# Layer 3 of a four-layer graph network: the projection by seven half-width products for each pair of graphs, and attention scores masked in place

## The chip, the core and the metric

The kernel runs on one core of one Trainium2 chip, in one launch, with no arithmetic on the host. The metric is the device time of that core in microseconds (us), taken as the median of several runs. Engines are named as the profile names them: PE is the matrix engine (TensorE) and PEld its weight loads, DVE is VectorE, ACT is ScalarE, POOL is GpSimd, SP is the engine that issues most of the DMAs.

## The reference

`x` holds 128 graphs of 128 nodes with 256 features (f32), `adj` their 128x128 adjacency (here only 0 and 1). Four layers follow one another, and each ends in `x = layernorm(x + layer(x, adj))`:

```
layer 0: four scores  (x * a_k) @ x.T  chosen by adj == 1..4, leaky relu, softmax, @ x
layer 1: relu(x @ W_upd + mean over incoming edges of (x @ W_msg) + bias)
layer 2: three GRU steps; each: m = h @ weight[i]; aggr = A.T @ m; h = gru_cell(aggr, h)
layer 3: Wh = h @ W                                  # W is 256x256
         e  = leaky_relu(Wh @ a1 [:, None] + Wh @ a2 [None, :])
         alpha = softmax(where(adj > 0, e, -1e9)); out = elu(alpha @ Wh)
```

The change lies in layer 3.

## The kernel before

**Tiling.** The 128 graphs go through in 32 groups of `G = 4`. A tile holds the four graphs of a group; features come in `KC = 2` chunks of 128. For each group the Python code records all operations of `loading`, `layer0`, `layer1`, `gru` (three steps) and `layer3`. It issues none of them at once: each record is an `Op` with its engine, its buffers and what it must follow. Every instruction is therefore issued from one line (L232 in the profile), and groups in the profile are told apart by the names of their tiles.

**The planner.** After recording, a list scheduler (lines 1064 to 1163) simulates the five engines with fixed costs (`pe_cost`, `dve_cost` and so on) and at each moment picks, among the operations that can start, the one with the earliest due time. Due times come from `paced`: the group's number times `PERIOD`, plus the stage's entry in `TIMES`, plus corrections for the first six groups (`HEAD`) and the last six (`TAIL`). `EAGER` and `RUSH` move single operations forward, `HOP`, `PE_HOP`, `SLACK` and `DMA_SLACK` are the delays that it assumes between an operation and its consumer. What comes out is only an order for each engine's queue. On the chip each engine follows its queue strictly, so an operation that isn't ready holds up all that stands behind it on its engine. Several groups are under way at once: while one is in layer 3, later ones are in layer 0, in layer 1 and in the GRU.

**Buffers.** Tiles with the same tag share memory (`tile_of(tag, ..., bufs)`). Eight PSUM banks exist: four under `ps`, four under `gate`. `LENT` and `LAST` let the first and the last groups use tags that stand idle then.

**Products of f32 data** are two passes on PE, each with its own weight load, so the profile counts two matmuls where the code has one. Two parts of the kernel already replace eight block products by seven: the GRU's gates (`gate`, with sums made by `sums`) and layer 1 (lines 701 to 736). There one PSUM region `sums` is built up by successive products, and between two of them an ACT or DVE instruction copies the state so far (`snapshot`). The next product onto `sums` has to wait for that copy.

**Layer 3 before.** `w3x` is 128 x 2 x 258: for each chunk the two columns W@a1 and W@a2 and the 256 columns of W, all with their mean over the features taken off, so that only the scale of the preceding layer norm is left to apply. For each graph two matmuls of 258 columns add up in one bank (line 964), and one ACT instruction multiplies by `rstd` and writes `wh` (line 968). `rstd` comes from `statistics(x3)`: `bn_stats` and `bn_aggr` on DVE, then POOL's power -0.5 (tile `norm`); `x3` is the same data in the other orientation, brought through DRAM, so PE can make the products before `rstd` is there. Column 1 of `wh` is turned into rows through DRAM (tile `e`); ACT's leaky relu adds column 0; POOL fills a second tile `alpha3` with -1e9, and DVE copies `e` into it where `m_gt` (adj > 0) is set. Softmax, the product with `wh`, elu, residual and the final layer norm follow.

The last group (`end`) is taken in two halves and gets its rows by a PE transpose instead of DRAM.

Of the kernel before, what the change touches and what calls it, by code (L numbers as in the profile page):

```python
# [9 lines left out]
U8 = mybir.dt.uint8  # L10
# [8 lines left out]
def kernel(  # L19
# [266 lines left out]
    def sp_cost(op, n, out, ins, pointers, sums):  # L286
# [7 lines left out]
    engines = (PE, DVE, ACT, POOL, SP)  # L294


    PERIOD = 80.86253
    EAGER, RUSH = 5.0884, 1.2432
    HOP, PE_HOP, SLACK, DMA_SLACK = 0.1014, 0.0400, 0.1471, 0.9854
    STAGES = ("loading", "layer0", "layer1", "step0", "step1", "step2", "layer3")  # L300
    TIMES = {
        "loading": ((-258.6487, -221.2981), (-177.7494, -380.8362),),
        "layer0": ((-168.3552, -133.3064), (-133.3096, -106.9608),),
        "layer1": ((-54.7884, -31.0927), (-31.3632, 1.9381),),
        "step0": ((1.0169, 6.5128), (2.0472, 18.0997), (16.3112, 40.9206),),
        "step1": ((47.0157, 58.4871), (54.6617, 81.1755), (64.0140, 96.5891),),
        "step2": ((103.0883, 125.4009), (124.8396, 134.0628), (117.2682, 150.2660),),
        "layer3": ((180.1358, 214.4429), (215.7571, 242.5671),),
        "weights": ((-169.3721, -63.5307), (-339.2026, -166.3094), (66.3971, -238.7909), (-41.6293, -259.0106), (11.0405, -48.3179), (-169.5807, -0.3718), (-340.4637, 8.4156),),
    }  # L310
    HEAD = (
        (-117.215, -459.664, -34.333, -29.161, 1.563, 32.989, 16.116),
        (1.845, -18.257, -21.556, 24.853, 21.190, -0.454, 36.615),
        (-212.928, -33.522, 22.746, 10.256, 10.342, 13.022, 18.440),
        (-257.587, 42.115, 8.229, 7.910, 18.207, 9.248, -2.588),
        (-39.284, 3.397, 16.065, 1.469, 3.447, 5.718, 2.966),
        (-103.261, -31.186, -1.392, -17.316, -0.422, 9.872, 6.232),
    )
    TAIL = (
        (218.880, -30.061, -19.516, -24.870, -14.301, 14.485, 9.628),  # L320
        (355.667, -8.045, -0.184, 12.567, 6.874, -3.896, -23.536),
        (108.002, 3.414, -6.453, -11.126, -2.010, -5.080, -2.710),
        (401.812, -59.141, -23.770, -14.732, -25.938, -6.000, 51.631),
        (550.661, -48.436, -51.059, -2.941, 57.600, 48.509, 200.181),
        (353.049, 27.888, 2.032, 49.745, 45.095, 76.448, 165.620),
    )

    def spread(start, end, pe_only=False):
# [31 lines left out]
    ident = tile_of("ident", [P, P])  # L360
    ident.buf.tile = ident_tile
    neg_half = tile_of("neg_half", [P, G])

    hu_tiles = [work.tile([P, 2 * D + 1], F32, tag=f"hu{k}", name=f"hu{k}") for k in range(2)]
    for hu_tile in hu_tiles:
# [9 lines left out]
    c_gi = tile_of("c_gi", [P, NL, KC, 3 * D])  # L375

    w3x = tile_of("w3x", [P, KC, 2 + D])

    w_ul = tile_of("w_ul", [P, 3, D])
    w_sh = tile_of("w_sh", [P, 3, 3, P])  # L380
# [2 lines left out]
    def weights():  # L383

        POOL.memset(neg_half, -0.5)
        nats, wnat = [], []
        for src, tag, bufs in ((w_ih, "hT", 6), (w_hh, "rest", 4)):
            for g in range(0, NGC, 2):
# [110 lines left out]
                PE.matmul(ps[:, : 2 + D], mean, w3x[:, c, :], start=(c == 0), stop=(c == KC - 1))  # L499
        for c in range(KC):  # L500
            DVE.tensor_sub(w3x[:, c, :], w3x[:, c, :], ps[:, : 2 + D])
        early(6)


# [67 lines left out]
    def softmax(alpha, tag, quick, tile=tile_of):  # L572

        n = alpha.shape[1]
        nmax = tile_of(f"nmax_{tag}", [P, n], 2)
        DVE.tensor_reduce(nmax, alpha, AX.X, OP.max, negate=True)
        rs = tile_of(f"rsum_{tag}", [P, n], 2)
        for b in range(n):
            ACT.activation(
                alpha[:, b, :], alpha[:, b, :], AF.Exp, bias=nmax[:, b : b + 1], scale=1.0,  # L580
                accum_out=rs[:, b : b + 1],
            )
        rinv = tile_of(f"rinv_{tag}", [P, n], 2)
# [110 lines left out]
    def layer1(g, s):  # L694
        x1, a_f, xT = s.x1, s.a_f, s.x1T

        s.m_gt = tile_of("m_gt", [P, G, N], 3, U8)
        POOL.tensor_scalar(s.m_gt, a_f, 0.0, None, op0=OP.is_gt)
        s.a_ne = tile_of("a_ne", [P, G, N], 3, BF16)
        DVE.tensor_scalar(s.a_ne, a_f, 0.0, None, op0=OP.not_equal)  # L700
        t = tile_of("xd", [P, 2, 3, N])
# [69 lines left out]
    def gru(g, s):  # L771
# [166 lines left out]


    LAST = {  # L940
        "wh": ("x_in", 1), "e": ("alpha0", 1), "alpha3": ("x_blocks", 1),
        "probT_3": ("probT_0", 1), "xd": ("x1T", 1),
    }

    def layer3(g, s, first, last):


        n = last - first
        end = g == NG - 1
        names = LAST if first else {}  # L950
        two, three = ("2b", "3b") if first else ("2", "3")

        def tile(tag, shape, bufs=1):
            tag, bufs = names.get(tag, (tag, bufs))
            return tile_of(tag, shape, bufs)

        x3 = s.x3 if n == G else s.x3[:, first:last]
        shift, rstd = statistics(x3, two)
        wh = tile("wh", [P, n, 2 + D])
        for b in range(n):  # L960
            ps = bank()
            with PE:
                for c in range(KC):
                    PE.matmul(
                        ps[:, : 2 + D], s.rT[c][:, (first + b) * N : (first + b + 1) * N], w3x[:, c, :],
                        start=(c == 0), stop=(c == KC - 1),
                    )
            ACT.mul(wh[:, b, :], ps[:, : 2 + D], rstd[:, b : b + 1])


        f = tile("e", [P, 4 * n, 32])
        e = f.rearrange("p (k b) c -> p b k c", [P, n, 4, 32], b=n)
        if end:
            ps = bank()
# [3 lines left out]
            rows = [ps[:, b * N : (b + 1) * N].rearrange("p (k c) -> p k c", c=32) for b in range(n)]  # L978
        else:
            z = tile_of("z_f", [P, 32])  # L980
            DVE.transpose(z, wh[:, :, 1:9])
            way = tile_of("way_f", [16, 32], 4, F32, dram)
            SP.dma_start(out=way, in_=z.rearrange("(m r) c -> r m c", [8, 16, 32], r=8)[0])
            SP.dma_start(out=f, in_=way.partition_broadcast(P))
            rows = [e[:, b] for b in range(n)]
        alpha = tile("alpha3", [P, n, N])
        POOL.memset(alpha, NEG3)
        for b in range(n):
            leaky(e[:, b], rows[b], wh[:, b, 0:1])
        BLOCKS = "p b (k c) -> p b k c"  # L990
# [201 lines left out]
```

## Time and profile before

| | |
|---|---|
| median of 3 runs | 2675.43 us (2675.09 to 2675.49) |
| the profiled execution | 2673.91 us |
| its span, first to last instruction | 2672.1 us |
| mean granted TensorE clock | 0.997 of full |
| PE / PEld busy | 2626.9 us (98%) / 2265.7 us (85%) |
| DVE / ACT / POOL busy | 2216.7 (83%) / 1790.2 (67%) / 1659.3 us (62%) |
| layer-3 projection, 480 of its f32 passes | 124.3 us busy as a group |
| mean DMA rate | 107 GB/s |

Durations below come from the profiled execution. The profile's *busy* of PE counts from a matmul's start to its modelled end, and matmuls overlap in the array, so a row's mean (381 ns for a pass of 256 columns) is longer than the distance at which such passes follow each other. That distance has to be read from start times in the timeline. "Idle before" is the time that an engine stood still before a group's instructions, with what ended it.

### The profile page before, as it was taken

Reading aid. Unit: us, or ns where it says so; the run is one execution under the profiler, and the core shown is the slowest. Engines: PE = TensorE matmul, PEld = TensorE weight load, DVE = VectorE, ACT = ScalarE, POOL = GpSimd, SP = SyncE. Lnnn points to the kernel's source line nnn. Section 1 sums busy time; section 2 is a strip of 40 time slices with the busy share of each in tenths; the row PEclk is TensorE's granted clock in tenths of the full one; section 3 lists DMA queues with packets and bytes.
Section 4 is the critical chain, followed back from the end, with each engine's and each line's share of the span. In section 5 each row is a group of like instructions: output and inputs, shape, how many; then the busy total and the mean of one; then the engine's idle time right before and its main releaser. Section 6 shows DMA issues by size and latency. Waiting matters only on the chain.

```text
span 2672.1 us, 44288 instructions
## 1 busy us (share of the span) xinstructions
PE 2626.9 (98%) x13700; PEld 2265.7 (85%) x13700; DVE 2216.7 (83%) x5386; ACT 1790.2 (67%) x4330; POOL 1659.3 (62%) x1536
## 2 busy tenths in 40 slices
PE   8999999999999999999999999999999999999996
PEld 6788888888888888888888888888888888888885
DVE  6887888888888888888888898888898888888877
ACT  4555766666776676776676766666776677657666
POOL 6456666655676655676665676656666656666452
PEclk9999999999999999999999999999999999999999
DMA  6545544555555555555555555555554545435431
GB/s 138 106 86 103 123 96 106 120 102 111 117 117 111 113 106 115 108 116 112 112 110 114 107 115 113 110 112 115 107 123 103 111 103 120 108 75 109 92 82 45
DMA packets 1317389, 286.83 MB, mean 107 GB/s; under 512 B 1068193, under 2 KB 1313057, under 8 KB 1317153
## 3 DMA queue, kind: packets, MB, share of 16 engines
q1 hardware_dynamic: 1314704, 281.63, 51.0%
q10 hardware_dynamic: 2448, 2.36, 0.4%
q8 instruction: 110, 1.80, 0.3%
q14 instruction: 127, 1.03, 0.1%
HBM read 168.44 MB, written 115.41 MB: 106 GB/s over the span
## 4 chain that ended last, share of the span: by engine, by line
PE 90%; DVE 5%; ACT 2%; DMA 1%; issue 1%; SPq 1%; POOL 0%; POOLq 0%; ACTq 0%; DVEq 0%
PE gate L232 62%; PE ps L232 28%; SPq L232 1%; DVE z L232 0%; DVE st L232 0%; DVE t_m L232 0%; DVE t_d L232 0%; ACT xs L232 0%; ACT xb L232 0%; DVE rest L232 0%; DVE xb L232 0%; DVE hu L232 0%; DVE alpha L232 0%; DVE t_z L232 0%; DVE xd L232 0%
## 5 line engine op out<-in xcount | busy, mean ns | idle before, releaser
L232 POOL TENSOR_TENSOR t_r<-t_r,t_i 128x512 f32<-128x512 f32 x186 | 244.4, 1326 | 204.5 <-ACT t_i L232 167.2
L232 PE MATMUL gate<-t_h,w_hhT 128*128 128x256 f32 x1152 | 343.8, 381 | 3.1 <-ACT t_z L232 2.3
L232 PE MATMUL gate<-t_h,w_sh 128*128 128x256 f32 x1152 | 338.8, 382 | 1.8 <-ACT q L232 0.5
L232 PE MATMUL gate<-hT,w_hhT 128*128 128x256 f32 x1152 | 336.6, 383 | 1.1 <-ACT x_in L232 0.6
L232 POOL TENSOR_TENSOR t_h<-hT 128x256 f32<-128x256 f32 x188 | 145.4, 791 | 308.4 <-DVE hT L232 241.0
L232 PE MATMUL gate<-t_m,c_gi 128*128 128x256 f32 x1116 | 331.6, 379 | 0.0
L232 PE MATMUL gate<-t_m,w_sm 128*128 128x256 f32 x1116 | 328.2, 379 | 0.1
L232 PE MATMUL gate<-agT,c_gi 128*128 128x256 f32 x1116 | 326.3, 380 | 0.5 <-ACT t_r L232 0.2
L232 POOL TENSOR_TENSOR t_d<-hT,t_n 128x512 f32<-128x512 f32 x192 | 260.2, 1366 | 40.1 <-ACT t_n L232 38.4
L232 ACT ACTIVATE q<-gate,bhn 128x256 f32<-128x256 f32 x372 | 176.7, 475 | 126.8 <-PE gate L232 120.8
L232 PE MATMUL ps<-xs,xT 128*128 128x256 f32 x1024 | 242.9, 381 | 5.4 <-ACT xs L232 5.4
L232 PEld LDWEIGHTS gate<-t_h,w_sh 128*128 128x128 f32 x1152 | 213.2, 190 | 40.9 <-ACT t_r L232 5.5
L232 PEld LDWEIGHTS gate<-t_h,w_hhT 128*128 128x128 f32 x1152 | 215.6, 190 | 37.3 <-ACT t_z L232 4.5
L232 PEld LDWEIGHTS gate<-hT,w_hhT 128*128 128x128 f32 x1152 | 213.7, 190 | 36.4 <-DVE t_i L232 4.8
L232 PEld LDWEIGHTS gate<-t_m,w_sm 128*128 128x128 f32 x1116 | 211.6, 190 | 29.9 <-ACT t_i L232 0.8
L232 PEld LDWEIGHTS gate<-t_m,c_gi 128*128 128x128 f32 x1116 | 211.3, 190 | 30.2 <-ACT t_i L232 1.2
L232 PEld LDWEIGHTS gate<-agT,c_gi 128*128 128x128 f32 x1116 | 210.6, 190 | 30.7 <-ACT agT L232 1.4
L232 POOL TENSOR_TENSOR norm<-norm,neg_half 128x4 f32<-128x4 f32 x128 | 157.2, 1228 | 111.1 <-DVE norm L232 76.6
L232 PEld LDWEIGHTS ps<-xs,xT 128*128 128x128 f32 x1024 | 194.2, 191 | 34.6 <-ACT xs L232 7.7
L232 ACT COPY t_r<-gate 128x256 f32<-128x256 f32 x279 | 103.1, 369 | 177.8 <-PE gate L232 177.5
L232 POOL TENSOR_SCALAR mk<-a_f 128x512 uint8<-128x512 f32 x120 | 186.6, 1564 | 7.0 <-DVE alpha L232 3.3
L232 ACT COPY t_z<-gate 128x256 f32<-128x256 f32 x288 | 105.8, 367 | 126.1 <-PE gate L232 124.4
(265 smaller groups left out, 7035.0 us busy)
## 6 DMA issues: line engine op xcount, KB each, us to landing
way<-z SPq DMA_DIRECT2D x188, 256.0 KB, 2.5
way_h<-z SPq DMA_DIRECT2D x126, 256.0 KB, 2.4
hn<-way_h SPq DMA_DIRECT2D x504, 64.0 KB, 2.5
x_blocks<-in_x_dram SPq DMA_DIRECT2D x248, 64.0 KB, 2.4
x_in<-in_x_dram SPq DMA_DIRECT2D x31, 512.0 KB, 4.2
way_p<-z SPq DMA_DIRECT2D x62, 256.0 KB, 2.4
probT<-way_p SPq DMA_DIRECT2D x248, 64.0 KB, 2.4
xc<-way SPq DMA_DIRECT2D x124, 128.0 KB, 3.0
```

The lines of the kernel that those rows point to most:

```text
L232: getattr(self.engine, name)(*[a.real() if isinstance(a, View) else a for a in args], **{k: a.real() if isinstance(a, View) else a for k, ...
```

## The change

For all groups but the last, the eight products of 258 columns in a group become fourteen of 129 (`M3 = 1 + D // 2`). For two graphs and two chunks, the activations form a 2x2 block matrix `a11, a12, a21, a22` (graph, chunk), and the two halves of `w3x` another. Four POOL instructions for each group form sums of activations in a tile under the tag `xd` (the fourth overwrites `a21` in `rT`); four DVE instructions in `weights` form sums of weights once, in `w3s`. For each pair of graphs, seven matmuls write two banks. Four ACT instructions take `sums` out at four states, each scaled by `rstd`, straight into `wh`; three DVE instructions add the other products, scaled too. Three of the four ACT instructions stand between two matmuls onto `sums`.

The scores lose their second tile: `alpha3` and POOL's filling of it go; the mask is turned round (`m_no`, adj <= 0), and DVE writes -1e9, broadcast from a small tile `neg3`, into `e` itself. Softmax then works on `e`, whose rows lie in blocks of 32 (except in the last group). The tables and constants of the planner have other values. With them the order of all queues can change.

```diff
-    PERIOD = 80.86253
-    EAGER, RUSH = 5.0884, 1.2432
-    HOP, PE_HOP, SLACK, DMA_SLACK = 0.1014, 0.0400, 0.1471, 0.9854
+    PERIOD = 80.11372
+    EAGER, RUSH = 2.6344, 0.7143
+    HOP, PE_HOP, SLACK, DMA_SLACK = 0.0400, 0.1378, 0.0735, 0.0000
...
@@ weights
+        DVE.memset(neg3[0], NEG3)
...
+        b11, b12, b21, b22 = [w3x[:, c, e : e + M3] for c in range(KC) for e in (0, M3)]
+        DVE.tensor_sub(w3s[:, 0], b12, b11)
+        DVE.tensor_sub(w3s[:, 1], b22, w3s[:, 0])
+        DVE.tensor_sub(w3s[:, 2], b22, b12)
+        DVE.tensor_sub(w3s[:, 3], b21, w3s[:, 1])
@@ softmax
-        DVE.tensor_reduce(nmax, alpha, AX.X, OP.max, negate=True)
+        DVE.tensor_reduce(nmax, alpha, AX.X if len(alpha.shape) == 3 else AX.XY, OP.max, negate=True)
@@ layer1
-        s.m_gt = tile_of("m_gt", [P, G, N], 3, U8)
-        POOL.tensor_scalar(s.m_gt, a_f, 0.0, None, op0=OP.is_gt)
+        s.m_no = tile_of("m_no", [P, G, N], 3, U8)
+        POOL.tensor_scalar(s.m_no, a_f, 0.0, None, op0=OP.is_le)
@@ layer3
-        for b in range(n):
-            ps = bank()
...
-            ACT.mul(wh[:, b, :], ps[:, : 2 + D], rstd[:, b : b + 1])
+        if end:
+            for b in range(n):
+                ps = bank()
...
+                ACT.mul(wh[:, b, :], ps[:, : 2 + D], rstd[:, b : b + 1])
+        else:
+            pairs = [r.rearrange("p (h j n) -> p h j n", [P, 2, 2, N], h=2, j=2) for r in s.rT]
+            a11, a12, a21, a22 = [pairs[c][:, :, j] for j in range(2) for c in range(KC)]
+            t = tile_of("xd", [P, 3, 2, N])
+            POOL.tensor_add(t[:, 0], a21, a22)
+            POOL.tensor_sub(t[:, 1], t[:, 0], a11)
+            POOL.tensor_sub(t[:, 2], a12, t[:, 1])
+            POOL.tensor_sub(a21, a11, a21)
+            for h in range(2):
+                shared, other = bank(), bank()
+                sums, second, third = shared[:, :M3], shared[:, M3 : 2 * M3], other[:, :M3]
+                data = [[pairs[c][:, h, j] for c in range(KC)] for j in range(2)]
...
+                def scaled(cols, j, half, rush=0.0):
+                    b = 2 * h + j
+                    ACT.mul(wh[:, b, half * M3 : (half + 1) * M3], cols, rstd[:, b : b + 1])
+                    ops[-1].rush = rush
+
+                def more(cols, j, half):
+                    b = 2 * h + j
+                    part = wh[:, b, half * M3 : (half + 1) * M3]
+                    DVE.scalar_tensor_tensor(part, cols, rstd[:, b : b + 1], part, op0=OP.mult, op1=OP.add)
+
+                product(sums, data[0][0], w3x[:, 0, :M3], first=True)
+                scaled(sums, 0, 0, 1.0)
+                product(second, data[0][1], w3x[:, 1, :M3], last=True)
+                product(sums, t[:, 1, h], w3s[:, 1])
+                scaled(sums, 0, 1, 1.0)
+                more(second, 0, 0)
+                product(third, t[:, 0, h], w3s[:, 0], first=True)
+                product(sums, data[1][0], w3s[:, 2])
+                scaled(sums, 1, 1, 1.0)
+                more(third, 1, 1)
+                product(sums, data[1][1], w3s[:, 3], last=True)
+                scaled(sums, 1, 0)
+                product(third, t[:, 2, h], w3x[:, 1, M3:], last=True)
+                more(third, 0, 1)
...
-        alpha = tile("alpha3", [P, n, N])
-        POOL.memset(alpha, NEG3)
         for b in range(n):
             leaky(e[:, b], rows[b], wh[:, b, 0:1])
-        DVE.copy_predicated(
-            alpha.rearrange(BLOCKS, c=32), s.m_gt[:, first:last].rearrange(BLOCKS, c=32), e
-        )
-        pT, rinv = softmax(alpha, three, end, tile)
+        no_edge = s.m_no[:, first:last]
+        DVE.copy_predicated(
+            e, no_edge if end else no_edge.rearrange(BLOCKS, e.shape, c=32), neg3[end].to_broadcast(e.shape)
+        )
+        pT, rinv = softmax(e, three, end, tile)
@@ LENT, group 1
-            "x_blocks": ("t_z", 1), "x_in": ("t_i", 1), "adj_in": ("alpha3", 1), "alpha0": ("e", 1),
+            "x_blocks": ("t_z", 1), "x_in": ("t_i", 1), "adj_in": ("agT", 2), "alpha0": ("e", 1),
```

More of the change, by code (lines that the diff above doesn't have):

```diff
@@ L294 @@
     engines = (PE, DVE, ACT, POOL, SP)
-    PERIOD = 80.86253
-    EAGER, RUSH = 5.0884, 1.2432
-    HOP, PE_HOP, SLACK, DMA_SLACK = 0.1014, 0.0400, 0.1471, 0.9854
+    PERIOD = 80.11372
+    EAGER, RUSH = 2.6344, 0.7143
+    HOP, PE_HOP, SLACK, DMA_SLACK = 0.0400, 0.1378, 0.0735, 0.0000
     STAGES = ("loading", "layer0", "layer1", "step0", "step1", "step2", "layer3")
     TIMES = {
[L302 to L309, printed above, removed]
+        "loading": ((-249.6079, -212.0678), (-113.8090, -332.9345),),
+        "layer0": ((-168.8692, -133.2780), (-133.5219, -104.5405),),
+        "layer1": ((-55.3795, -33.1012), (-31.5377, 2.8510),),
+        "step0": ((-11.9427, 20.7603), (1.2145, 16.3006), (16.0065, 40.8857),),
+        "step1": ((47.7399, 59.7962), (45.3548, 87.7173), (62.6142, 97.1739),),
+        "step2": ((98.7693, 129.3523), (123.5816, 134.7948), (115.9123, 150.4592),),
+        "layer3": ((180.4921, 214.2708), (215.9126, 243.4544),),
+        "weights": ((-226.2091, -120.9666), (-321.9048, -194.9663), (-100.0366, -399.7056), (-173.6798, -398.3343), (-25.1752, -58.0656), (-193.8768, -11.7763), (-492.1222, -10.8166),),
@@ L310 @@
     }
     HEAD = (
[L312 to L317, printed above, removed]
+        (-109.736, -470.462, -53.540, -36.016, -24.006, 34.656, 5.249),
@@ L318 @@
+        (14.077, -3.774, -16.434, 3.961, 17.588, -4.390, 0.673),
+        (-215.480, 47.555, 16.443, 9.977, 11.006, 21.354, 27.407),
+        (-276.144, 11.272, 5.278, -7.933, -1.824, 24.093, -15.039),
+        (-53.675, -8.128, 18.441, -6.523, -0.531, 21.056, 8.709),
+        (-97.191, -39.499, -5.564, -3.961, 1.883, 10.914, 25.090),
     )
     TAIL = (
-        (218.880, -30.061, -19.516, -24.870, -14.301, 14.485, 9.628),
-        (355.667, -8.045, -0.184, 12.567, 6.874, -3.896, -23.536),
-        (108.002, 3.414, -6.453, -11.126, -2.010, -5.080, -2.710),
@@ L323 @@
-        (401.812, -59.141, -23.770, -14.732, -25.938, -6.000, 51.631),
-        (550.661, -48.436, -51.059, -2.941, 57.600, 48.509, 200.181),
-        (353.049, 27.888, 2.032, 49.745, 45.095, 76.448, 165.620),
+        (200.431, -16.725, 3.742, 3.796, 11.256, 10.903, 17.562),
+        (310.831, -20.088, 1.464, 20.508, 6.830, 10.759, -28.108),
+        (128.223, 24.862, 15.678, 9.322, 2.180, 9.262, 9.186),
+        (423.903, -21.531, 8.580, 0.748, -3.281, 30.156, 102.119),
+        (638.546, -59.992, -46.471, 18.310, 61.378, 90.947, 213.613),
@@ L326 @@
+        (276.437, 42.631, 7.771, 60.198, 81.212, 211.570, 154.252),
     )
@@ L362 @@
     neg_half = tile_of("neg_half", [P, G])
+    neg3 = [tile_of("neg3", [P, 1, 1, 1])]
+    neg3.append(neg3[0][:, 0])
     hu_tiles = [work.tile([P, 2 * D + 1], F32, tag=f"hu{k}", name=f"hu{k}") for k in range(2)]
@@ L377 @@
     w3x = tile_of("w3x", [P, KC, 2 + D])
+    M3 = 1 + D // 2
+    w3s = tile_of("w3s", [P, 4, M3])
     w_ul = tile_of("w_ul", [P, 3, D])
@@ L940 @@
     LAST = {
-        "wh": ("x_in", 1), "e": ("alpha0", 1), "alpha3": ("x_blocks", 1),
+        "wh": ("x_in", 1), "e": ("alpha0", 1),
         "probT_3": ("probT_0", 1), "xd": ("x1T", 1),
@@ L959, in layer3, with product @@
         wh = tile("wh", [P, n, 2 + D])
-        for b in range(n):
-            ps = bank()
[L962 to L966, printed above, removed]
-                    )
-            ACT.mul(wh[:, b, :], ps[:, : 2 + D], rstd[:, b : b + 1])
+        if end:
+            for b in range(n):
+                ps = bank()
+                with PE:
+                    for c in range(KC):
+                        PE.matmul(
+                            ps[:, : 2 + D], s.rT[c][:, (first + b) * N : (first + b + 1) * N], w3x[:, c, :],
+                            start=(c == 0), stop=(c == KC - 1),
+                        )
[12 more added lines that the diff above has]
+                data = [[pairs[c][:, h, j] for c in range(KC)] for j in range(2)]
+                def product(cols, stationary, weights, first=False, last=False):
+                    PE.matmul(cols, stationary, weights, start=first, stop=last, skip_group_check=True)
+                def scaled(cols, j, half, rush=0.0):
[20 more added lines that the diff above has]
+                more(third, 0, 1)
@@ L971, in layer3 @@
+        BLOCKS = "p b (k c) -> p b k c"
         f = tile("e", [P, 4 * n, 32])
-        e = f.rearrange("p (k b) c -> p b k c", [P, n, 4, 32], b=n)
         if end:
+            e = f.rearrange("p (b k) c -> p b (k c)", [P, n, N], b=n)
             ps = bank()
@@ L977, in layer3 @@
                     PE.transpose(ps[:, b * N : (b + 1) * N], wh[:, b, 1:2].to_broadcast([P, N]), ident)
-            rows = [ps[:, b * N : (b + 1) * N].rearrange("p (k c) -> p k c", c=32) for b in range(n)]
+            rows = [ps[:, b * N : (b + 1) * N] for b in range(n)]
         else:
+            e = f.rearrange("p (k b) c -> p b k c", [P, n, 4, 32], b=n)
             z = tile_of("z_f", [P, 32])
@@ L985, in layer3 @@
             rows = [e[:, b] for b in range(n)]
-        alpha = tile("alpha3", [P, n, N])
-        POOL.memset(alpha, NEG3)
         for b in range(n):
             leaky(e[:, b], rows[b], wh[:, b, 0:1])
-        BLOCKS = "p b (k c) -> p b k c"
+        no_edge = s.m_no[:, first:last]
         DVE.copy_predicated(
-            alpha.rearrange(BLOCKS, c=32), s.m_gt[:, first:last].rearrange(BLOCKS, c=32), e
+            e, no_edge if end else no_edge.rearrange(BLOCKS, e.shape, c=32), neg3[end].to_broadcast(e.shape)
         )
-        pT, rinv = softmax(alpha, three, end, tile)
+        pT, rinv = softmax(e, three, end, tile)
         normalise(x3, shift, rstd, int(end))
```

## The prediction

> **What bounds the kernel now.** I read the page's header first, then a table by stretches, then the timeline of PE, then the waits.
>
> ```profile
> PE 2626.9 (98%) x13700; PEld 2265.7 (85%) x13700; DVE 2216.7 (83%) x5386; ACT 1790.2 (67%) x4330; POOL 1659.3 (62%) x1536
> ```
>
> PE is busy nearly throughout. Three stretches and one period of the steady part, by stretch: length, PE busy (count), PEld, DVE, ACT, POOL, granted clock, DMA share, GB/s.
>
> ```profile
> 0.00:60.00 60.00, 47.96 (x205) 35.28 (x206) 39.28 (x95) 29.20 (x63) 39.97 (x42) 1.00 0.71 149
> 60.00:2620.00 2560.00, 2546.68 (x13343) 2205.34 (x13342) 2142.64 (x5200) 1730.97 (x4188) 1606.68 (x1482) 1.00 0.52 108
> 837.91:918.51 80.60, 80.60 (x425) 70.34 (x425) 67.87 (x166) 55.52 (x136) 52.37 (x49) 1.00 0.54 111
> ```
>
> PE is idle for 12.0 us at the start, for 2560.00 - 2546.68 = 13.3 us in the long middle, and not at all in a period of the steady part, at full clock. That PE is busy does not prove that it is dense, since a matmul's end is modelled. So I went to start times. Lines of PE's timeline (start, length, group):
>
> ```profile
> 13.79 1.04 PE L232 MATMUL ps<-ident,rest 128*128 128x128 f32 x8
> 14.66 0.67 PE L232 MATMUL ps<-wh,hT 128*128 128x256 f32 x2
> ...
> 857.70 0.22 PE L232 MATMUL ps<-a_ne,xb 128*128 128x128 bf16 x1
> 857.75 0.28 PE L232 MATMUL ps<-a_ne,rest 128*128 128x128 bf16 x2
> 857.86 1.09 PE L232 MATMUL ps<-w3x,rT 128*128 128x258 f32 x4
> ...
> 1518.74 1.03 PE L232 MATMUL ps<-w3x,rT 128*128 128x258 f32 x4
> 1519.61 0.59 PE L232 MATMUL gate<-t_m,w_sm 128*128 128x256 f32 x2
> 1520.04 1.03 PE L232 MATMUL ps<-w3x,rT 128*128 128x258 f32 x4
> 1520.91 1.02 PE L232 MATMUL gate<-hT,w_hhT 128*128 128x256 f32 x4
> ```
>
> Four passes of 258 columns take 1519.61 - 1518.74 = 0.87 us, 0.2175 each; two of 256 take 0.43, 0.216 each; three bf16 passes of 128 columns take 857.86 - 857.70 = 0.16 to 0.17, 0.056 each. One group needs 176 f32 products (352 passes) and 72 bf16 passes, 424 in all, and the period shows 425. 352 x 0.216 + 72 x 0.056 = 80.06 us out of 80.60. PE is at its floor: the period can shrink only by PE work, and whatever makes PE wait is paid in full.
>
> **Matmuls: removed and added.** Out go 8 x 2 = 16 passes of 258 columns: 4 x 0.87 = 3.48 us for each group. In come 14 x 2 = 28 passes of 129 columns, each with a load of its own. No f32 product of that width stands in the trace. From below, half of a 258-column pass: 0.109. From above, should loads not follow each other faster than their own length, the 190 ns of PEld's rows. The nearest rows lie near the lower end: eight f32 transposes of 128 columns, each with its load, take 14.66 - 13.79 = 0.87, 0.109 each. They are one pass and not two, so I also looked at loads of true two-pass products that start after a pause (PEld's timeline):
>
> ```profile
> 8.72 0.30 PEld L232 LDWEIGHTS ps<-wh,hT 128*128 128x128 f32 x2 [0.95 <-ACT hT L232]
> ```
>
> Two loads in 0.30, each 0.19 long: the second started 0.11 after the first. I take 0.110, so 28 x 0.110 = 3.08. The gain is 3.48 - 3.08 = 0.40 us for each group, and 31 groups (the last keeps the old way) give 12.4 us. At 0.124 a pass nothing would be left; at 0.19 the change would lose (5.32 - 3.48) x 31 = 57 us.
>
> A rule of the Trainium skill speaks against this term. "TensorE: Matmul & The Clock Gate", section "Back-to-back issue gap", says that a stream of weight loads and matmuls of 128 columns settles at about 81 ns a pair, because the loads are part of the pace. This trace has such a stream, in bf16, at 56 ns. Were the page's 81 to 56 put on the new passes, an estimate from that page would give 28 x 0.110 x 81/56 = 4.46 us, a loss of 0.98 for each group and 2706 us in all. I stay with the rows.
>
> **Copies out of PSUM, scaled.** ACT loses four instructions of 0.48 (128x258, `wh`) and gets eight of 129 columns; the nearest row, 128x128 from PSUM into `e`, has 0.36. 8 x 0.37 - 4 x 0.48 = +1.0 us. DVE gets six multiply-adds from PSUM. These rows lie on both sides:
>
> ```profile
> L232 DVE SCALAR_TENSOR_TENSOR xb<-ps,fac,hu 128x256 f32<-128x256 f32 x128 | 60.1, 479 | 1.0
> L232 DVE SCALAR_TENSOR_TENSOR fac<-ps,fac 128x1 f32<-128x1 f32 x128 | 18.4, 154 | 1.4
> ```
>
> Halfway is 0.32, so +1.9 us. DVE comes to 69.8 and ACT to 56.5 of 80.2: neither becomes the bound, so I price this at nothing, with PE's other groups as the cover. If the cover fails, the price is that of a late copy, below.
>
> **POOL.** Four sums of 128x256, like layer 1's four (0.74, 0.79, 0.77, 0.92 us): +3.2, less the filling of `alpha3` (0.53): +2.7, to 55.1 of 80.2. They stand in POOL's queue after the last sum into `rT` and wait for DVE's last write of `rT`; behind them stand the GRU's sums `t_h` and `t_r` of other groups. POOL has 25 us free in a period, so again nothing. The filling waited 5.7 us for `wh` in the period shown; that wait goes, but POOL has slack and it isn't worth time.
>
> **Scores.** One predicated copy, one maximum, four exponentials and one transpose as before, over rows in blocks of 32, which the leaky relu already has (0.39 for 128x128, the plain exponential 0.40). Between a little below nothing and 0.1 us on DVE; nothing on PE. `neg3` and four sums of weights cost DVE some 1.1 us once, near 53 us; PE idles there anyway. `m_no` costs what `m_gt` did. No DMA is added. SP issues the same `way_f` and `e` transfers, perhaps in other places; with `DMA_SLACK` at nothing the planner no longer allows about 1 us after a landing.
>
> **The waits added.** This is the dear part. Before, the projection waited for nothing but `rT`: in the period at 838 us PE made it at 857.9 to 860.1, and ACT came for it only at 869.0, since `rstd` was ready at 868.1. Now the second product onto `sums` waits for ACT's copy, and that for `rstd`. So the chain moves behind the statistics: DMA of `x3`, DVE's `bn_stats`, POOL's power. Three such copies for each pair, six for each group, 186 in all; behind each waiting product stands the whole PE queue. An uncovered one can be read from layer 1, which has the same chain:
>
> ```profile
> 57.18 0.70 PE L232 MATMUL ps<-w_um,x1T 128*128 128x256 f32 x2 [0.90 <-DVE hu L232]
> ```
>
> 0.90 us each. But covered ones are the rule. PE's waits over 60 to 2620 us (total, times, longest) have for layer 1's `hu`, with its six for each group:
>
> ```profile
> PE ps L232 <- DVE hu L232: 1.8, 4, 0.9
> PE ps L232 <- ACT hu L232: 1.6, 3, 0.9
> ```
>
> 3.4 us for the whole middle, none of it between 838 and 1905. I bound the new waits by 0 and 3.4 at layer 1's rate, and take 2, as the new order may cover the edges better or worse. The 13.3 us of middle idleness can move either way with a new order; within ±7 (half of it) I take 0.
>
> **The sum**, on the profiled span: 2672.1 - 12.4 + 2.0 = 2661.7. The profiled execution was 1.8 above its span, and the median 1.5 above that execution: 2661.7 + 3.3 = **2665.0 us**. With the ends: 2675.4 - 12.4 - 7 = 2656 to 2675.4 - 12.4 + 3.4 + 7 = 2673.
>
> **Rivals.**
>
> *A late scale makes PE wait (slower).* One mechanism: `rstd` or a copy isn't there when PE's queue reaches the next product onto `sums`, because the planner now assumes landings and hops shorter. For it: that PE was already waiting on ACT and DVE at the edges, and before the change ACT waited 5.3 us in six places for `norm` ahead of `wh`, waits that PE would now share. Against it: none of those cost PE anything in the steady part, and there the order repeats exactly. It decides from 12.4 / 31 = 0.40 us of waiting for each group; at 0.65 the time is 2675.4 + 31 x 0.25 = 2683; at one uncovered copy for each group (0.90) it is 2691. Chance 0.17.
>
> *Nothing is left (same).* Passes come out at 0.120 instead of 0.110, or one copy in twenty is uncovered: 28 x 0.010 x 31 = 8.7, or 9 x 0.90 = 8 us given back, 2671 to 2675. For it: the width is at the point where load and columns are equally long, with no margin in either. Chance 0.10.
>
> *The new order also removes idleness (faster still).* If half of the middle idleness goes and no wait is added: 2675.4 - 12.4 - 7 = 2656. I count it within my forecast; the chance of the forecast with it is 0.73.
>
> *Loads set the pace.* At 0.19 a pass, 2675 + 57 = 2732. The load row above speaks plainly against it; it is inside the 0.17.
>
> **How the numbers follow.** Some 0.2% (5.4 us) is about what a measurement can tell from no change. Faster 0.73, same 0.10, slower 0.17. The likeliest case's own range is 2656 to 2673. To hold 8 in 10 it reaches, above, to the late scale at 0.65 us for each group (2683), and, below, to the rest of the middle idleness won back less 2 us of waits: 2675.4 - 12.4 - 11.3 = 2652.
>
> **What the changed profile would show.** Right: a steady period near 80.2 us with PE still full and about 437 matmuls; products from `w3x` and `w3s` with `rT` and `xd` whose two passes stand 0.22 apart from the next; PE waits on `wh` of a few us. Wrong: `PE ps <- ACT wh` or `<- POOL norm` above some 12 us in total; a spacing above 0.25 for a product; DVE or PEld ending PE's idle time in every period; or an idle middle that grows for reasons outside layer 3, which would put it on the planner's new order and not on the products.

## The result, and the profile after

The changed kernel takes 2796.16 us (median of four runs, 2795.10 to 2796.85), the kernel before 2675.26 beside it: a ratio of 1.0454 (95%: 1.0441 to 1.0466). The forecast was 2665.0, with a range that ended at 2683. The profiled span is 2793.2 us, 121.1 more than before.

First the header of the changed kernel's page, then its table by stretches (length, PE busy and count, PEld, DVE, ACT, POOL, granted clock, DMA share, GB/s).

```profile
span 2793.2 us, 45332 instructions
...
PE 2669.2 (96%) x14072; PEld 2264.9 (81%) x14072; DVE 2287.6 (82%) x5577; ACT 1826.1 (65%) x4454; POOL 1720.4 (62%) x1627
```

```profile
60.00:2740.00 2680.00, 2594.94 (x13777) 2209.72 (x13777) 2218.35 (x5401) 1771.83 (x4322) 1674.37 (x1579) 1.00 0.50 103
921.00:1005.00 84.00, 82.40 (x446) 71.68 (x445) 70.25 (x178) 57.43 (x140) 54.81 (x53) 1.00 0.53 110
```

The long middle now has 2680.00 - 2594.94 = 85.1 us without PE, against 13.3. The clock is still full and every engine's share is lower or the same, so no engine has become the bound. Neighbouring groups make the same product some 84.5 us apart in the middle, where it was 80.60, and the pattern no longer repeats exactly.

The chain of work that ended last says who was waited for, first before, then after:

```profile
PE 90%; DVE 5%; ACT 2%; DMA 1%; issue 1%; SPq 1%; POOL 0%; POOLq 0%; ACTq 0%; DVEq 0%
PE 58%; DVE 19%; DMA 8%; ACT 7%; SPq 3%; issue 3%; POOL 3%; DVEq 0%; POOLq 0%; ACTq 0%
```

**Were the products dearer than thought?** Two of them, next to each other in a filled queue, from the timeline (start, length, group):

```profile
1503.15 0.39 PE L232 MATMUL ps<-w3x,xd 128*128 128x129 f32 x2
...
1503.37 0.39 PE L232 MATMUL ps<-w3x,rT 128*128 128x129 f32 x2
```

1503.37 - 1503.15 = 0.22 us for two passes, as forecast. If every product is counted with the distance at which it follows another in a filled queue, PE needs 2586 us for the operations before and 2576 for those after. From PE's first start to its last start there are 2660.7 - 4.7 = 2656 us before and 2783.0 - 4.6 = 2778 after. What work does not fill is called standing here: PE stood 70 us before and stands 203 now. The change of 122 in PE's own stretch is thus about -11 of work and +133 of standing. It is work that became no dearer: passes of 256 columns, by far the most, start 0.216 us apart in the median of either kernel.

**Where does PE stand?** Its waits between 60 and 2740 us (total, times, longest), some of the largest, and far below them those for the new copies:

```profile
PE gate L232 <- DVE t_i L232: 15.1, 18, 1.5
PE ps L232 <- ACT hu L232: 12.0, 20, 0.7
PE ps L232 <- DVE hu L232: 7.5, 15, 1.2
PE gate L232 <- DVE q L232: 7.4, 15, 1.3
...
PE ps L232 <- DVE wh L232: 1.4, 2, 1.2
...
PE ps L232 <- ACT wh L232: 0.3, 2, 0.2
```

These are waits of the GRU (`gate`) and of layer 1 (`hu`), parts that the change doesn't touch. One step back, among DVE's waits, is one that grew from 3.2 to 49.5 us (the line of before, then that of after):

```profile
DVE rest L232 <- DMA hn<-way_h: 3.2, 7, 1.3
DVE rest L232 <- DMA hn<-way_h: 49.5, 55, 2.4
```

`hn` is the GRU's state in the other orientation, brought through DRAM. How its lateness reaches PE is seen in the timeline at 1503 us:

```profile
1502.72 0.60 PE L232 MATMUL gate<-t_h,w_hhT 128*128 128x256 f32 x2
...
1503.65 0.69 DVE L232 TENSOR_TENSOR rest<-hn 128x512 f32<-128x512 f32 x1 [1.29 <-DMA hn<-way_h]
...
1504.26 0.68 DVE L232 TENSOR_TENSOR t_i<-gate,t_i 128x512 f32<-128x512 f32 x1
...
1505.00 0.70 PE L232 MATMUL gate<-hT,w_hhT 128*128 128x256 f32 x2 [1.24 <-DVE t_i L232]
```

DVE stood 1.29 us for a landing. Behind that instruction stood `t_i`, and no product into `gate` was under way after 1503.32 that it could have waited for. It started as DVE came free, and PE stood 1.24 us for `t_i`. A queue that is followed strictly hands a late transfer on to work that has nothing to do with it.

From this came the theory, **ORDER**: products, copies and scores cost what was forecast; the time was lost because the planner's new numbers put all five queues in another order, which the chip's delays don't let it keep. Its rivals: **LATE SCALE** (layer 3's copies wait for `rstd` and push everything behind them back) and **OPERATIONS** (the new instructions cost more than their own durations, in any order).

### The profile page after: what moved, and what is told of

Its sections match the earlier page's. It is cut to its first block, busy times and chain, and to the rows that moved or that the text cites. A ratio compares the mean times of both kernels' runs of the same rounds, so it can differ in the third digit from the quotient of the medians.

```text
span 2793.2 us, 45332 instructions
## 1 busy us (share of the span) xinstructions
PE 2669.2 (96%) x14072; PEld 2264.9 (81%) x14072; DVE 2287.6 (82%) x5577; ACT 1826.1 (65%) x4454; POOL 1720.4 (62%) x1627
## 4 chain that ended last, share of the span: by engine, by line
PE 58%; DVE 19%; DMA 8%; ACT 7%; SPq 3%; issue 3%; POOL 3%; DVEq 0%; POOLq 0%; ACTq 0%
PE gate L232 38%; PE ps L232 20%; DMA hn<-way_h 3%; SPq L232 3%; DVE rest L232 2%; DVE t_m L232 2%; DMA way_h<-z 2%; DVE t_d L232 2%; DVE xb L232 1%; DVE z L232 1%; DVE st L232 1%; ACT xb L232 1%; POOL t_r L232 1%; DVE hu L232 1%; DVE t_r L232 1%
## 5 line engine op out<-in xcount | busy, mean ns | idle before, releaser
L232 POOL TENSOR_TENSOR t_r<-t_r,t_i 128x512 f32<-128x512 f32 x186 | 255.8, 1386 | 378.1 <-ACT t_i L232 136.2
L232 PE MATMUL gate<-hT,w_hhT 128*128 128x256 f32 x1152 | 346.0, 385 | 14.2 <-DVE t_i L232 11.2
L232 POOL TENSOR_TENSOR t_h<-hT 128x256 f32<-128x256 f32 x188 | 138.5, 747 | 190.6 <-DVE hT L232 102.6
L232 PEld LDWEIGHTS gate<-t_h,w_hhT 128*128 128x128 f32 x1152 | 207.6, 190 | 53.2 <-ACT t_z L232 17.9
L232 PEld LDWEIGHTS gate<-t_h,w_sh 128*128 128x128 f32 x1152 | 205.5, 190 | 52.8 <-ACT t_r L232 12.7
L232 PEld LDWEIGHTS gate<-hT,w_hhT 128*128 128x128 f32 x1152 | 207.6, 191 | 43.6 <-DVE t_i L232 13.6
L232 POOL TENSOR_TENSOR norm<-norm,neg_half 128x4 f32<-128x4 f32 x128 | 142.4, 1113 | 151.3 <-DVE norm L232 146.8
L232 ACT ACTIVATE xs<-xT,acol 128x512 f32<-128x512 f32 x256 | 173.9, 718 | 21.4 <-DVE xT L232 12.8
```

The costliest lines, as they stand in the source:

```text
L232: getattr(self.engine, name)(*[a.real() if isinstance(a, View) else a for a in args], **{k: a.real() if isinstance(a, View) else a for k, ...
```

## The experiments

All in one table. "Own" is PE's work, counted with the start distances of filled stretches, so it is the same wherever the operations are; "stands" is what is left between PE's first and last start in each trace. The kernel before had 2673.8 to 2675.4 us beside these runs.

| run | operations | order | us | ratio (95%) | own | stands |
|---|---|---|---|---|---|---|
| before | before | before | 2675.3 | 1 | 2586 | 70 |
| after | after | after | 2796.2 | 1.0454 (1.0441-1.0466) | 2576 | 203 |
| a1_scale_at_hand | after, scale from elsewhere | after | 2787.9 | 1.0423 (1.0392-1.0453) | 2576 | 193 |
| a2_no_hn_landing | after, `hn` from elsewhere | after | 2759.4 | 1.0316 (1.0286-1.0346) | 2576 | 166 |
| a3_before_four_delays | before | four delays of after | 2799.1 | 1.0465 (1.0427-1.0502) | 2586 | 198 |
| a4_scores_only | before with the new scores | tables of before | 2733.2 | 1.0218 (1.0189-1.0248) | 2586 | 129 |
| b1_new_tables | after | found anew | 2699.5 | 1.0099 (1.0082-1.0116) | 2576 | 105 |
| b2_period_only | before | `PERIOD` 80.9 | 2778.0 | 1.0388 (1.0368-1.0409) | 2586 | 174 |
| b3_before_dma_slack_0 | before | `DMA_SLACK` 0 | 2773.0 | 1.0370 (1.0349-1.0390) | 2586 | 169 |
| b4_after_longer_delays | after | longer delays | 2797.5 | 1.0461 (1.0440-1.0482) | 2576 | 202 |
| c1_one_stall | after | b1, 14 moved | 2695.8 | 1.0081 (1.0064-1.0098) | 2576 | 103 |
| c2_many_moves | after | b1, 263 moved | 2690.4 | 1.0063 (1.0043-1.0083) | 2576 | 99 |
| c3_more_moves | after | c2, 168 more | 2686.1 | 1.0040 (1.0026-1.0054) | 2576 | 92 |

**a1: the scale at hand.** The order of the queues is that of the changed kernel; layer 3's copies scale by a resident column instead of `rstd`, so they wait for products alone.

```diff
-                    ACT.mul(wh[:, b, half * M3 : (half + 1) * M3], cols, rstd[:, b : b + 1])
+                    ACT.mul(wh[:, b, half * M3 : (half + 1) * M3], cols, rstd[:, b : b + 1].instead(bhn[:, :1]))
...
-                    DVE.scalar_tensor_tensor(part, cols, rstd[:, b : b + 1], part, op0=OP.mult, op1=OP.add)
+                    DVE.scalar_tensor_tensor(part, cols, rstd[:, b : b + 1].instead(bhn[:, :1]), part, op0=OP.mult, op1=OP.add)
```

> The changed kernel, every queue in its order, but the copies and multiply-adds of layer 3 scale by a resident column (bhn) instead of rstd, so the seven-product chain no longer waits for the statistics (the scale itself is wrong by that, only the time is read). Theory LATE SCALE (my rival on record: rstd or a copy is late and PE waits): most of the 121 us go, to 2700 or less. Theory ORDER (the new order of all queues has no reserve against the chip's real delays, whichever operation they belong to): no more than 10 us, 2786 to 2797; in the changed profile PE waits for copies into wh only 1.7 us in all.

2787.9 us: some 8 of the 121 go with the wait for the scale (roughly, as the intervals of this run and the changed kernel overlap), 113 stay. LATE SCALE isn't the cause.

**a2: no wait for `hn`.** Same order again; what splits `hn` into its bf16 parts reads a resident tile, so the aggregation runs on other data and DVE never waits for this landing.

```diff
-        by.tensor_sub(rest, h, h.high())
+        by.tensor_sub(rest, whole, high)
...
+                    still = c_gi[:, 0, 0, : G * P].rearrange("p (b n) -> p b n", [P, G, P], b=G)
-                    split_up[c] = split(turning[c], DVE)
+                    split_up[c] = split(turning[c], DVE, still)
```

> The changed kernel, every queue in its order, but DVE's split of the GRU state and PE's aggregation read a resident tile instead of hn, which the DMA still writes (so the GRU's aggregate is of other data). In the changed profile DVE waited 49.5 us in 55 places for the landing of hn; before the change 3.2 us. Theory LANDINGS (the planner, told that a landing costs nothing more, puts DVE on data that isn't there, and that is the loss): 2796 less 50 to 100, 2700 to 2746. Theory ORDER: landings of hn are one of several late arrivals, and what one of them gives back the next one takes: 2755 to 2785 (I estimate 25 us, from replaying the queues' order with delays that fit both profiles). LATE SCALE: 2796.

2759.4 us, 37 less: PE's standing falls from 203 to 166, and `gate <- DVE t_i`, which led PE's waits, is gone from their head (line numbers are shifted by the edit):

```profile
PE ps L242 <- ACT hu L242: 11.3, 18, 0.7
PE gate L242 <- ACT t_z L242: 7.7, 14, 0.9
PE gate L242 <- ACT t_r L242: 7.4, 18, 1.1
```

Late landings of `hn` are thus three tenths of the loss (37 of 121), within what ORDER expected and short of the 50 to 100 us that LANDINGS expected. One way in which they reach PE is the path shown at 1503 us. What leads PE's waits now is engines.

**a3: the delays alone, not one operation changed.**

```diff
-    HOP, PE_HOP, SLACK, DMA_SLACK = 0.1014, 0.0400, 0.1471, 0.9854
+    HOP, PE_HOP, SLACK, DMA_SLACK = 0.0400, 0.1378, 0.0735, 0.0000
```

> The kernel before with one line of the change: HOP, PE_HOP, SLACK, DMA_SLACK = 0.0400, 0.1378, 0.0735, 0.0000. The operations are those of before, only the order can differ. LATE SCALE, or any theory in which the seven products cost the time: 2675. ORDER: above 2740; my estimate, from the same replay, 2815, as bad as the whole change.

2799.1 us: the kernel before, with all its old products and its second score tile, loses as much as the changed kernel did. In its middle PE is idle for 2560.00 - 2474.47 = 85.5 us, and DVE's and PE's waits for landings are there too:

```profile
60.00:2620.00 2560.00, 2474.47 (x12710) 2090.50 (x12709) 2085.41 (x4980) 1674.61 (x3992) 1531.98 (x1427) 1.00 0.52 104
```

```profile
PE ps L232 <- DMA probT<-way_p: 11.9, 16, 1.3
...
DVE rest L232 <- DMA hn<-way_h: 28.9, 37, 2.9
```

OPERATIONS isn't needed to explain a loss of this size. That it contributes nothing isn't shown yet.

**a4: the scores alone**, with the tables of before (the second tile, its filling and `m_gt` go as in the diff of the change).

> The kernel before, with its own tables and constants, and only the scores edit: no alpha3, mask turned round and written into e, softmax on e. It takes 31 fillings off POOL and adds nothing to any engine. If what an edit costs is read from its instructions: 2675 within 3. ORDER: the planner, fed other operations with tables fitted to the old ones, gives another order for everything, and the time rises though work falls: 2700 to 2750, my estimate 2725.

2733.2 us: a tile, a POOL instruction for each group and their waits are taken out, nothing costly is put in, and the kernel is 58 us slower. `hn` is hardly waited for (1.4 us), so this isn't the landings' reserve. PE stands 129 us instead of 70. That is what tables fitted to one set of operations would do to another, but this run alone doesn't tell the order's share from that of the scores' own new dependencies. The runs with unchanged operations (a3, b2, b3) do.

**b1: other tables for the changed kernel.** All 139 numbers of the planner are others, chosen so that the order stands also where a result or a landing comes some tenths of a us later than the planner assumes.

```diff
-    PERIOD = 80.11372
-    EAGER, RUSH = 2.6344, 0.7143
-    HOP, PE_HOP, SLACK, DMA_SLACK = 0.0400, 0.1378, 0.0735, 0.0000
+    PERIOD = 80.205836
+    EAGER, RUSH = 2.815612, 1.384098
+    HOP, PE_HOP, SLACK, DMA_SLACK = 0.088479, 0.150195, 0.133854, 0.436599
...
```

> All operations of the changed kernel; only the planner's 139 numbers (PERIOD, EAGER, RUSH, the four delays, TIMES, HEAD, TAIL) are others, chosen so that the order stands also where a result or a landing comes some tenths of a us later than the planner thinks. ORDER (the loss is the order of the queues, which had no reserve against real delays; products and scores cost what was forecast): 2665 to 2690 us, idle middle of PE 13 to 30 us instead of 85, DVE's waits for landings of hn under 10 us instead of 49.5, PE's waits for gate by DVE's t_i under 5 instead of 15.1, and periods near 80.3 us somewhere in the middle. OPERATIONS (the products, the copies with their scale or the scores are dearer in themselves, whatever the order): the time stays above 2740, and PE's idle middle above 50 us.

2699.5 us: with the same operations, 97 of the 121 us come back. The time is 10 us above the range that ORDER gave, and far below OPERATIONS' 2740. Table by stretches, then PE's largest waits, then DVE's for `hn`:

```profile
60.00:2620.00 2560.00, 2525.86 (x13604) 2188.02 (x13603) 2195.04 (x5347) 1745.11 (x4280) 1663.83 (x1566) 1.00 0.52 108
```

```profile
PE ps L232 <- DVE hu L232: 12.5, 20, 0.8
PE ps L232 <- ACT xs L232: 3.4, 2, 2.9
...
DVE rest L232 <- DMA hn<-way_h: 6.6, 12, 1.2
```

PE is idle for 34.1 us of the middle instead of over 78 in the same stretch of the changed kernel, and DVE's wait for `hn` is about an eighth of what it was, as ORDER expected. The idle middle (30 us at most) and the distance of successive groups, 81.2 us (near 80.3), miss what ORDER expected of them. One wait is left that repeats.

**b2: one number of the kernel before moved by 0.05%.**

```diff
-    PERIOD = 80.86253
+    PERIOD = 80.9
```

> The kernel before with PERIOD 80.9 instead of 80.86253, all delays and operations as they were. ORDER in its narrow form (only delays that are set too short do harm): 2670 to 2685 us. ORDER in its wide form (the tables hold for one order alone, and any other order of the same work stands worse, also with the old delays): 2730 to 2770 us, with PE waiting more on DVE and ACT than on landings, and DVE's waits for hn well below the 28.9 us of the run with the four new delays.

2778.0 us, 103 more, beyond what even ORDER's wide form expected; operations and delays are those of before. Table by stretches, then DVE's wait for `hn`, then PE's largest waits:

```profile
60.00:2620.00 2560.00, 2495.25 (x12869) 2123.27 (x12868) 2062.94 (x5040) 1673.38 (x4040) 1535.39 (x1443) 1.00 0.51 105
```

```profile
DVE rest L232 <- DMA hn<-way_h: 1.4, 3, 1.0
```

```profile
PE gate L232 <- ACT t_z L232: 17.9, 27, 3.4
PE gate L232 <- ACT agT L232: 9.3, 22, 1.3
PE ps L232 <- ACT wh L232: 6.3, 3, 4.5
```

The middle is idle for 64.8 us and the groups follow at 83.4 instead of 80.6 us, yet `hn` is waited for less than before. So late landings aren't the loss here: engines wait for engines, because the same work stands in another order.

**b3: the reserve for landings alone**, in the kernel before.

```diff
-    HOP, PE_HOP, SLACK, DMA_SLACK = 0.1014, 0.0400, 0.1471, 0.9854
+    HOP, PE_HOP, SLACK, DMA_SLACK = 0.1014, 0.0400, 0.1471, 0.0000
```

> The kernel before with DMA_SLACK 0 instead of 0.9854, nothing else. If the landings' reserve is the whole of the loss of the four delays: 2790 to 2800 us, as with all four. If the short delays of the engines have a share of their own: 2750 to 2780, DVE's waits for hn near the 28.9 us seen with all four.

2773.0 us, as the second reading expected, and here the landings are late: DVE's wait for `hn` is in the region of a3's, and PE waits for another transfer itself.

```profile
DVE rest L232 <- DMA hn<-way_h: 20.7, 32, 1.8
```

```profile
PE ps L232 <- DMA probT<-way_p: 8.0, 9, 1.5
```

b2 and b3 lose about the same, 103 and 98 us, by different waits.

**b4: longer delays for the changed kernel**, its other tables as they were.

```diff
-    HOP, PE_HOP, SLACK, DMA_SLACK = 0.0400, 0.1378, 0.0735, 0.0000
+    HOP, PE_HOP, SLACK, DMA_SLACK = 0.15, 0.1, 0.2, 0.3
```

> The changed kernel with HOP, PE_HOP, SLACK, DMA_SLACK at 0.15, 0.1, 0.2, 0.3 instead of 0.0400, 0.1378, 0.0735, 0, all other tables as they were. If short delays alone are the fault: below 2700 us. ORDER in its wide form: the waits for landings shrink to under 20 us on DVE, but the tables do not fit the new order, and the time is 2755 to 2785.

2797.5 us. DVE's wait for `hn` falls from 49.5 to 9.0 us, as expected, but nothing of the time is won: it lies 12 us above the range that ORDER's wide form gave. PE now waits elsewhere, as the second list shows, once for 8.8 us at 241 us, where a new product of layer 3 waits for ACT's `wh`:

```profile
DVE rest L232 <- DMA hn<-way_h: 9.0, 16, 1.2
```

```profile
PE gate L232 <- ACT t_z L232: 16.5, 18, 3.2
PE ps L232 <- ACT wh L232: 9.6, 3, 8.8
PE gate L232 <- DVE t_r L232: 8.0, 13, 1.2
```

The narrow form of ORDER (delays set too short, and nothing else) falls with b2 and b4. What stands is the wide form: the due times in the tables and the delays belong together, and every other order that was tried without a new fit, whichever number brought it about, took 58 to 124 us more.

**c1: one repeating wait of b1.** Between 990 and 2050 us PE stands once in each period for DVE's `hu`. The timeline around one of them:

```profile
1408.87 1.35 POOL L232 TENSOR_TENSOR t_r<-t_r,t_i 128x512 f32<-128x512 f32 x1 [7.87 <-ACT t_i L232]
1409.01 1.75 DVE L232 SCALAR_TENSOR_TENSOR t_r<-t_r,q 128x512 f32<-128x512 f32 x1
1410.69 0.68 DVE L232 TENSOR_TENSOR t_i<-gate,t_i 128x512 f32<-128x512 f32 x1
...
1411.29 0.41 DVE L232 TENSOR_TENSOR hu<-hu,ps 128x256 f32<-128x256 f32 x1
...
1411.75 0.48 PE L232 MATMUL ps<-w_ul,x1T 128*128 128x256 f32 x1 [0.79 <-DVE hu L232]
```

DVE's update `t_r<-t_r,q` takes 1.75 us here and 0.67 where POOL is quiet. It starts 0.14 us after a two-input instruction of POOL and is done 0.54 after that one's end (1410.76 against 1410.22). c1 puts the update behind `t_i` and `hu`, in 14 places:

```diff
+        if late.engine is DVE and named(late, "scalar_tensor_tensor", "t_r", "t_r", "q"):
...
+                    plan.insert(mine[1], plan.pop(k))
```

> b1_new_tables with 14 DVE instructions moved, 12 of them the same one in successive groups: the update t_r<-t_r,q stands behind the sums into t_i and hu that followed it, instead of ahead of them. In b1 PE stood 0.95 us for that hu in each period between 990 and 2050 us, because the update there took 1.75 us instead of 0.67. ORDER: the stall goes, 12 x 0.95 = 11 us at most, the time is 2688 to 2694, the period in the middle 80.3 to 80.6 instead of 81.2. If stalls of that size are absorbed or replaced by another: 2698 or more.

2695.8 us (runs from 2693.3 to 2698.0), between the two expectations, and not clearly apart from b1, since the intervals overlap. The same place in c1:

```profile
1409.01 0.67 DVE L233 TENSOR_TENSOR t_i<-gate,t_i 128x512 f32<-128x512 f32 x1
1410.11 0.42 DVE L233 TENSOR_TENSOR hu<-hu,ps 128x256 f32<-128x256 f32 x1 [0.43 <-ACT hu L233]
1410.45 0.68 DVE L233 SCALAR_TENSOR_TENSOR t_r<-t_r,q 128x512 f32<-128x512 f32 x1
```

```profile
1411.23 0.59 PE L233 MATMUL gate<-hT,w_hhT 128*128 128x256 f32 x2
1411.85 0.67 PE L233 MATMUL gate<-t_h,w_sh 128*128 128x256 f32 x2
1412.63 0.70 PE L233 MATMUL ps<-w_um,x1T 128*128 128x256 f32 x2
```

The long wait is gone and the update takes 0.68. But the products at 1411.85 and 1412.63 are now 0.62 and 0.78 after those ahead of them, where 0.43 would do: short stands came for the long one, and the period falls from 81.2 to 80.8 and not to 80.3.

**c2 and c3: many places at once.** The list of moves is written out in the kernel; each is "this instruction goes ahead of that one in the same queue", with what it needs.

```diff
+    MOVES = (
+        ...
+    )
+    for late, early in MOVES:
+        ...
```

> b1_new_tables with 263 instructions moved forward in their queues by one to five places, at the places where PE, or something PE waited for later, stood behind an instruction that nobody needed yet. No operation and no buffer is changed. ORDER: PE's standing time between its products, 94.6 us in b1, falls by 15 to 34 us: 2664 to 2684 us. If the rest above the kernel before belongs to the new operations: 2690 or more.

> c2_many_moves with another 168 instructions moved forward in their queues, chosen by the places where its trace shows PE standing; the moves now also reckon that a two-input instruction of DVE and one of POOL wait for each other's end but for 0.14 us, as the traces show. No operation and no buffer is changed. ORDER: 2673 to 2685 us, as PE's standing time falls further. If what is left above the kernel before belongs to the new operations: 2690 or more.

2690.4 and 2686.1 us. Both miss ORDER's range. c2 misses it by 6 us and lies just inside the other one, from 2690 up, where the rest was to be put down to the operations; c3 lies between the two, 1 us above ORDER's. PE's standing fell from 105 to 99 in c2, where 15 to 34 us less was looked for, and to 92 in c3; in c1, moved instructions met new neighbours, and that may be so here. The intervals of neighbouring steps overlap; those of b1 and c3 are apart (1.0082 at least against 1.0054 at most), with the same work. c3's table, in the stretch of b1's, then PE's waits between 60 and 2640 us, the two largest and the one for the new copies:

```profile
60.00:2620.00 2560.00, 2530.58 (x13656) 2196.60 (x13655) 2210.48 (x5360) 1753.15 (x4295) 1672.78 (x1573) 1.00 0.52 108
```

```profile
PE ps L233 <- ACT hu L233: 8.6, 14, 1.2
PE ps L233 <- DVE hu L233: 4.0, 9, 1.1
...
PE ps L233 <- ACT wh L233: 2.3, 5, 1.0
```

So by order alone, 110 of the 121 us are won back with the operations untouched. The remaining 11 us are again standing: 92 against 70, less the 11 of saved work. Whose standing it is, isn't shown. By start distances in c3's trace, 6.7 of the 92 us stand right ahead of products of 129 columns, which wait for the new copies and sums, so the new operations may hold a part of it. No version here beats the kernel before. Whether an order exists in which the saved work shows, stays open.

Not tried: the changed operations with the tables of before, the products alone in the kernel before, and sums of layer 3 in a tile of their own.

## Why the prediction was wrong

**PE is the bound, and what makes it wait is paid in full.** Right, as far as the runs tell: 133 us more of standing less 11 of work make 122, and the span grew by 121.1. Standing is counted as what work leaves over, so this sum must close; that the time was lost by waiting is seen in PE's idle middle, which grew from 13.3 to 85.1 us.

**The products.** Right. 0.22 us for two passes of 129 columns; of the 868 passes, the middle half starts 0.110 to 0.112 us before the next, 0.111 in the median. PE's work falls by about 11 us, against 12.4, as 0.111 is a little more than the 0.110 taken. The rule of the Trainium skill that the prediction weighed against this row ("TensorE: Matmul & The Clock Gate", section "Back-to-back issue gap") would have made the term a loss; the measurement decides for the row.

**Copies and sums.** ACT's scaled copy lasts 370 ns (0.37 forecast), DVE's multiply-add 344 (0.32), POOL's sums 0.76 to 0.83 us. Priced at nothing. No run takes them out; what a1 shows is that waiting for their scale costs some 8 us in this order.

**The waits added.** 2 us taken, 1.7 found (`ps <- DVE wh` and `ps <- ACT wh`). The rival *late scale* needed 0.40 us for each group, 12.4 in all, to decide; with 1.7 us of direct waits, and some 8 by a1, it falls. *Loads set the pace* falls with the spacing. *Nothing is left* and *less idleness* were not what happened.

**The step that failed** is the sentence "The 13.3 us of middle idleness can move either way with a new order; within ±7 (half of it) I take 0." By the prediction's own measure it was +72 us (13.3 to 85.1 of PE's idle middle), by start distances +133 us of standing in the whole kernel. Two things were wrong in it. The size of the idleness before was taken as the measure of what a new order can change. But it says nothing of what an order can lose: b2 loses 103 us by a step of 0.05% in one table. Nor is it all that an order could win, since by start distances PE stood 70 us before. And the table edits got no term but this zero; a3 shows that four of their numbers, put into the kernel before, cost 124 us, as much as the whole change. The remark on `DMA_SLACK` stood in the text and was priced only through `rstd`. The prediction named the sign by which this would be known (idleness that grows for reasons outside layer 3), but gave it no rival and no share of the range. An exactly repeating pattern with no idle PE was in plain view; after a3 and b2 it can be read as a sign of an order fitted to its operations, and so as a warning.

## What to carry to other kernels

Where queues are ordered by a fitted planner, any edit of operations or tables is an edit of the whole order. Price it one-sidedly: the bound engine's standing is the most that can be won (70 us here, by start distances, and no run won any), while the loss went up to 124 us. To value such an edit, count the bound engine's own work by start distances and its standing apart from it; here the first said about -11 us and the second +133. To find what an order costs, run the old operations with the new tables before looking for faults in the new operations.

## What the runs showed of the hardware

**DVE's `t_r<-t_r,q` and POOL's `t_r<-t_r,t_i`, each with two inputs in SBUF, wait for each other nearly to the end.** In b1 the DVE instruction began 15 times while the POOL one was under way, and each time it was longer by the rest of POOL's instruction less 0.13 us. The other way round POOL's was longer by the rest of DVE's less 0.13 to 0.14 us (the middle half of 22 cases). The Trainium skill, "SBUF — State Buffer", section "SBUF: two separate sides", has the mechanism: the pair of ports that both use is held by whichever comes first, and the other is blocked. The trace agrees, but for those 0.13 to 0.14 us by which its records overlap. An order can trip over it: in the place shown for c1, a start 0.14 us behind POOL's cost DVE 1.08 us.

**Small delays, large sum.** From the end of an instruction in the record to the start of one that waited for it there are only 0.03 to 0.08 us in the median of the commonest pairs (in the changed kernel 0.033 from ACT to DVE, 0.055 from DVE to PE, 0.080 from DVE to POOL). A landing of `hn` takes 2.2 to 2.5 us from issue in the median of a run. Those that DVE stood for took 2.6 us from issue to DVE's start in the median, a quarter of them over 3.2 (72 in the changed kernel, a4, b1 and b2 together). No single delay is near 100 us. Small ones that repeat are: between 1360 and 1440 us of the changed kernel PE stands in six places, 0.39 to 0.67 us each, and so it goes on group after group.
